# A product of the identity beside each lead step of a recurrence

## The chip, the core and the metric

The kernel runs on one core of one Trainium2 chip, in one launch, in float32. The metric is the device time of one execution in microseconds. An execution is run several times; the number quoted is the median.

## What is computed

Three layers follow one another on an input of 4 images with 128 channels and 64 x 64 pixels: a deformable neighbourhood attention (kernel lines up to about 600), a recurrence and eight state-space layers that are the subject here, and a layer of routed experts. Cut to what matters, the middle reads:

```
...
# recurrence over 4096 positions, 4 images side by side, 128 channels
z = -1
for t in range(4096):
    z = tanh(0.5 * (norm(W x1)[t] + (V/2)^T z + shift))
    x2[t] = x1[t] + 0.5 * z + 0.5
# eight layers on x2, each with 256 inner channels and 16 states
dA, dBx = exp(dt * A), dt * xc * B
h[t] = dA[t] * h[t-1] + dBx[t]
y[t] = sum over states of h[t] * C[t]
...
```

The recurrence is written here as the kernel computes it; in the reference it is a sigmoid of the same sum.

## The kernel before

The five engines each run their own queue of instructions, in the order in which the program text issues them: the kernel's order is written out by hand (`tc.manual_schedule()`), and semaphores make an instruction wait for what it reads. TensorE does the products (a weight load and a matmul pass are separate instructions, shown as PEld and PE; a float32 product comes as two of each), VectorE (DVE) the scans, ScalarE (ACT) exponentials, tanh and copies, GpSimd (POOL) elementwise products, and SyncE (SP) issues the transfers.

**The recurrence.** The class `Recurrence` holds it. `step(t)` (line 656) does one position for all four images. With every 64th position (RT = 64) it takes up the next group: a product of the identity with 256 columns of wx (line 664) puts the group's input into the PSUM tile `p`. Then, at every position, a product of `vt` (128 x 128) with the four columns of the last `z` is added into four columns of `p` (line 669), and ScalarE takes the tanh of these into the next four columns of `z` (line 672). The next step's product needs that `z`, so the steps can't overlap. In the middle of a group `load` fetches the next group's inputs; after the last position of a group POOL adds `z` to `x1` (lines 678 and 679), and SP stores it as `x2`.

**The state-space layers.** `mamba` (line 727) works on pieces ("bodies") of 512 positions, one image and one layer each, in the order piece, layer, image. A body has 16 slots; in each, two scans of 512 positions run on VectorE (line 1031), with the exponentials (line 976) on ScalarE, the inputs `dBx` from TensorE into PSUM (line 998), the products with C on POOL (line 1047) and their sum by TensorE (line 1051). The PSUM tiles of `dBx` come from the pool `psx`, which has two buffers (line 754).

**The lead.** The layers need whole pieces of 512 positions of x2. So before the loop over bodies, the function runs `PRE` = 512 + 64 = 576 steps of the recurrence by themselves. Only then come the norms of the first bodies (lines 810 to 822, 1108, 1112), and the loop, in which the other 3520 steps are spread over the slots (`STEPS`).

Of the kernel before, what the change touches and what calls it, by code (L numbers as in the profile page):

```python
# [8 lines left out]
F32 = mybir.dt.float32  # L9
# [10 lines left out]
P = 128  # L20
# [25 lines left out]
TL = 512  # L46
# [680 lines left out]
def mamba(tc, ops, I, rec, x2_d, x3_d):  # L727
# [8 lines left out]
    nc = tc.nc  # L736
# [5 lines left out]
    with ExitStack() as ctx:  # L742
# [11 lines left out]
        psx = ctx.enter_context(tc.tile_pool(name="mpx", bufs=2, space=PSUM))  # L754
# [43 lines left out]
        def load(l):  # L798
            given = wp.tile([P, W_GIVEN], F32, tag="given", name="given")
            nc.sync.dma_start(out=given, in_=I["m_given"][l])  # L800
            weights[l] = given
# [354 lines left out]
                    pieces[what](who[k])  # L1156

        load(0)
        for t in range(PRE):
            rec.step(t)  # L1160
        for s in bodies[0:3]:
            for what in ("fetch", "mean", "var", "lnv", "rstd", "u"):
                pieces[what](s)
# [363 lines left out]
@with_exitstack  # L1527
def tile_kernel(ctx: ExitStack, tc: tile.TileContext, I, out):
    nc = tc.nc
    const = ctx.enter_context(tc.tile_pool(name="const", bufs=1))  # L1530
    dram = ctx.enter_context(tc.tile_pool(name="scratch", bufs=1, space=DRAM))
    nc.scalar.preload_act_table_set(EXP_LN)
    ops = Ops(nc, const)
    stats = const.tile([P, B * NBLK, 6], F32, name="stats")
    gating_w = gating_weights(tc, const, ops, I)
    x1_d = dram.tile([P, B, L], F32, name="x1_d")
    x2_d = dram.tile([P, B, L], F32, name="x2_d")
    x3_d = dram.tile([P, B, L], F32, name="x3_d")
    wx_d = dram.tile([P, B, L], F32, name="wx_d")

    with tc.manual_schedule():
        with ExitStack() as c:
            conv_layer(tc, ops, I, x1_d, wx_d, stats)
            rec = Recurrence(c, tc, ops, I, stats, wx_d, x1_d, x2_d)
            mamba(tc, ops, I, rec, x2_d, x3_d)
        experts(tc, ops, I, gating_w, x3_d, out)
# [89 lines left out]
```

## Time and profile before

| | |
|---|---|
| median of three runs | 15757.4 us (15743.53 to 15757.71) |
| the profiled execution | 15756.73 us, of which the span from first to last instruction is 15754.2 us |
| mean clock granted to TensorE | 0.966 of full speed |
| busy share of the span | PE 91%, DVE 87%, POOL 84%, ACT 76% |

A profile line of the page's list of groups is read so: line of the kernel, engine, operation, output tile <- input tiles, output shape <- input shape, number of instructions | busy time in us, mean of one in ns | idle time of that engine before them, and what ended it. For a weight load and a matmul, "128\*128" gives the rows and columns of the array in use. A line of the timeline gives the start, the time from the first start to the last end of a run of equal instructions, engine, line, and in brackets the idle time before them. A matmul's end is modelled, and counts the time in which its results are still in the pipeline. A line of the windows view gives a stretch of the span, then for each engine its busy time and its number of instructions, then the granted TensorE clock as a share of full speed, and the transfers.

The stages, by windows of the span:

| stretch, us | PE busy | DVE busy | ACT busy | POOL busy | clock |
|---|---|---|---|---|---|
| 1400 to 1600 (attention) | 182.19 | 147.62 | 150.52 | 94.29 | 0.94 |
| 1800 to 2000 (lead steps) | 139.26 | 0.00 | 41.82 | 5.04 | 0.50 |
| 2400 to 2600 (state-space layers) | 189.97 | 186.34 | 160.52 | 186.62 | 1.00 |

### The profile page before, as it was taken

Reading aid. Unit: us, or ns where it says so; the run is one execution under the profiler, and the core shown is the slowest. Engines: PE = TensorE matmul, PEld = TensorE weight load, DVE = VectorE, ACT = ScalarE, POOL = GpSimd, SP = SyncE. Lnnn points to the kernel's source line nnn. Section 1 sums busy time; section 2 is a strip of 40 time slices with the busy share of each in tenths; the row PEclk is TensorE's granted clock in tenths of the full one; section 3 lists DMA queues with packets and bytes.
Section 4 is the critical chain, followed back from the end, with each engine's and each line's share of the span. In section 5 each row is a group of like instructions: output and inputs, shape, how many; then the busy total and the mean of one; then the engine's idle time right before and its main releaser. Section 6 shows DMA issues by size and latency. Waiting matters only on the chain. (4 is left out here: it accounts for less than half of the span.)

```text
span 15754.2 us, 303022 instructions
## 1 busy us (share of the span) xinstructions
PE 14399.4 (91%) x120596; PEld 10805.1 (69%) x120596; DVE 13692.4 (87%) x14937; ACT 12014.9 (76%) x23591; POOL 13181.8 (84%) x9086
## 2 busy tenths in 40 slices
PE   6888779999999999999999999999999999989996
PEld 3444557777777777777777777777777777766664
DVE  8998039998999899998999899989998999999994
ACT  6888247887888878877788787878887888777773
POOL 4555039999999999999999999999999999999993
PEclk8999569999999999999999999999999999999998
DMA  0000012222222222222222222222222222222224
GB/s 22 22 22 22 15 50 99 104 98 105 97 97 104 101 102 101 99 103 97 103 104 96 104 98 100 104 100 104 98 97 101 101 104 101 98 103 95 98 101 168
DMA packets 423478, 1431.58 MB, mean 91 GB/s; under 512 B 204081, under 2 KB 204465, under 8 KB 290865
## 3 DMA queue, kind: packets, MB, share of 16 engines
q1 hardware_dynamic: 422064, 1412.21, 24.1%
q8 instruction: 952, 15.60, 0.4%
q14 instruction: 462, 3.78, 0.1%
HBM read 1353.33 MB, written 58.72 MB: 90 GB/s over the span
## 5 line engine op out<-in xcount | busy, mean ns | idle before, releaser
L1031 DVE TENSOR_TENSOR_SCAN hs<-dA,state,dBx 128x512 f32<-128x512 f32 x7168 | 8716.1, 1263 | 987.2 <-PE dBx L998 865.5
L1047 POOL TENSOR_TENSOR hs<-hs,Cb 128x2048 f32<-128x2048 f32 x2048 | 9296.0, 4539 | 166.2 <-POOL state L1044 1.3
L976 ACT ACTIVATE dA<-dt,A 128x512 f32<-128x512 f32 x7168 | 4728.8, 721 | 8.2 <-DVE hs L1031 2.0
L1051 PE MATMUL yT<-ident,hs 128*128 128x128 f32 x32768 | 4328.6, 276 | 8.5 <-POOL hs L1047 8.5
L1051 PEld LDWEIGHTS yT<-ident,hs 128*128 128x128 f32 x32768 | 3779.6, 144 | 773.3 <-issue 651.1
L998 PE MATMUL dBx<-diag,dtxT 64*128 64x128 f32 x57344 | 4187.2, 285 | 72.7 <-DVE hs L1031 46.9
L998 PEld LDWEIGHTS dBx<-diag,dtxT 64*128 64x128 f32 x57344 | 3511.2, 188 | 1027.3 <-issue 697.6
L672 ACT ACTIVATE z<-p 128x4 f32<-128x4 f32 x4096 | 711.4, 174 | 1573.2 <-PE p L669 1567.3
L669 PE MATMUL p<-z,vt 128*128 128x4 f32 x8192 | 1579.5, 263 | 239.5 <-ACT z L672 233.9
L669 PEld LDWEIGHTS p<-z,vt 128*128 128x128 f32 x8192 | 1350.5, 207 | 635.6 <-ACT z L672 378.4
L1019 POOL TENSOR_TENSOR hs<-Bb,dtx 128x512 f32<-128x512 f32 x1024 | 1276.0, 1281 | 5.6 <-PE yT L1051 4.8
L1031 DVE TENSOR_TENSOR_SCAN hs<-dAp,state,hs 128x512 f32<-128x512 f32 x1024 | 1228.6, 1262 | 0.0
L863 DVE SCALAR_TENSOR_TENSOR xc<-f,taps,xc 128x509 f32<-128x509 f32 (+2 forms) x1536 | 1130.5, 736 | 42.3 <-ACT tail L858 15.1
L964 DVE TENSOR_TENSOR diag<-f,i 128x512 f32<-128x512 f32 x1792 | 1157.2, 670 | 7.8 <-PE f L952 7.8
L1044 POOL COPY state<-hs 128x4 f32<-128x4 f32 x2048 | 389.6, 190 | 773.0 <-DVE hs L1031 617.3
L1129 ACT ACT_TABLE_LOAD x771 | 989.2, 1283 | 10.5
L278 DVE SCALAR_TENSOR_TENSOR acc<-qp,dww,acc 128x512 f32<-128x512 f32 x1184 | 887.0, 749 | 12.2
L976 ACT ACTIVATE dAp<-dt,A 128x512 f32<-128x512 f32 x1024 | 709.0, 692 | 209.9 <-DVE hs L1031 178.9
L878 PE MATMUL f<-u,given 128*128 128x512 f32 x1024 | 509.9, 620 | 333.5 <-ACT pos L1097 322.8
L854 ACT ACTIVATE xc<-f,edge,taps 128x1 f32<-128x1 f32 x1536 | 426.6, 350 | 450.2 <-POOL edge L839 449.9
L937 POOL TENSOR_TENSOR dtx<-dt,xc 128x512 f32<-128x512 f32 x512 | 651.8, 1273 | 11.9 <-ACT dt L931 11.9
L947 ACT COPY dtxT<-f 128x512 f32<-128x512 f32 x512 | 298.1, 582 | 384.1 <-PE f L944 384.1
(233 smaller groups left out, 16082.2 us busy)
## 6 DMA issues: line engine op xcount, KB each, us to landing
Cb<-c_d SPq DMA_DIRECT2D x1024, 1024.0 KB, 4.6
Bb<-c_d SPq DMA_DIRECT2D x256, 512.0 KB, 5.4
given<-in_m_given_dram SPq DMA_DIRECT2D x64, 640.0 KB, 5.9
slab<-in_w_dram SPq DMA_DIRECT2D x64, 512.0 KB, 9.9
x<-x_d SPq DMA_DIRECT2D x96, 256.0 KB, 4.2
x_d<-x SPq DMA_DIRECT2D x64, 256.0 KB, 2.2
c_d<-dbl SPq DMA_DIRECT2D x512, 32.0 KB, 1.6
xb<-in_x_dram SPq DMA_DIRECT2D x32, 256.0 KB, 3.0
```

The source lines that it names most:

```text
L278: nc.vector.scalar_tensor_tensor(rows(to), x, dww[:, t : t + 1], rows(o.acc), ALU.mult, ALU.add)
L669: nc.tensor.matmul(self.p[:, k, :], self.vt, self.before, start=False, stop=True, skip_group_check=True)
L672: nc.scalar.activation(self.z[:, k, :], self.p[:, k, :], AF.Tanh, scale=0.5)
L863: nc.vector.scalar_tensor_tensor(x, o.v[h][:, : TL - k], taps[:, o.l, h, DC - 1 - k : DC - k], x, ALU.mult, ALU.add)
L964: nc.vector.tensor_tensor(o.diag[:, sp], bt.unsqueeze(2).to_broadcast([P, NB, 64, 2]), i64.unsqueeze(1).unsqueeze(3).to_broadcast([P, NB, ...
L976: nc.scalar.activation(o.dA[j][:, k, :], o.dt[h], AF.Exp, scale=A[:, o.l, h, n : n + 1])
L998: nc.tensor.matmul(o.dBx[j][:, at : at + 64, :], o.dtxT[h][row, n, :], o.diag[row, sp, n], start=True, stop=True,)
L1019: nc.gpsimd.tensor_tensor(hs[:, k, :].rearrange("p (q n t) -> p q n t", n=NB, q=2), o.Bb[:, k, :].rearrange("p (q n t) -> p q n t", n=NB, ...
L1031: nc.vector.tensor_tensor_scan(hs[:, k, :], o.dA[j][:, k, :], hs[:, k, :] if sp == SP_B else o.dBx[j][:, :, k], state[:, o.l, o.b, h, s : ...
L1047: nc.gpsimd.tensor_tensor(hs, hs, o.Cb[f], ALU.mult)
L1051: nc.tensor.matmul(o.yT[:, n, :], x[:, n * P : (n + 1) * P], ops.ident, start=start and n == 0, stop=True, is_transpose=True, skip_group_c ...
L1129: return lambda o: nc.scalar.preload_act_table_set(name)
```

## The change

After each of the 576 lead steps, TensorE is given one more product: 32 columns of the identity as the weights, and the whole identity, 128 columns, as the data that moves through. The result goes to a corner of a tile `idle` in one of the two `dBx` buffers in PSUM. The tile is allocated once, ahead of the lead steps, and nothing reads it. The steps inside the loop over bodies are as before.

```diff
@@ -1156,8 +1156,13 @@
         load(0)
+
+        idle = psx.tile([P, 2, TL], F32, tag="dBx", name="idle")
         for t in range(PRE):
             rec.step(t)
+            nc.tensor.matmul(
+                idle[0:32, 0, 0:P], ops.ident[:, 0:32], ops.ident, start=True, stop=True
+            )
         for s in bodies[0:3]:
```

## The prediction

> **What bounds the kernel now.** I read the page first, for the stretch that the change touches.
>
> ```profile
> span 15754.2 us, 303022 instructions
> ...
> POOL 4555039999999999999999999999999999999993
> PEclk8999569999999999999999999999999999999998
> ...
> L672 ACT ACTIVATE z<-p 128x4 f32<-128x4 f32 x4096 | 711.4, 174 | 1573.2 <-PE p L669 1567.3
> L669 PE MATMUL p<-z,vt 128*128 128x4 f32 x8192 | 1579.5, 263 | 239.5 <-ACT z L672 233.9
> ```
>
> Each digit is a slice of 394 us. In the slices where POOL drops to 0 the clock of TensorE (PEclk) is at 5 to 6 tenths: these are the lead steps of the recurrence, which run alone. The windows view gives the clock and the load in the middle of them:
>
> ```profile
> 1800.00:2000.00 200.00, 139.26 (x469) 118.18 (x469) 0.00 (x0) 41.82 (x234) 5.04 (x8) 0.50 0.04 8
> ```
>
> The columns are length, busy time of PE, weight loads, DVE, ACT and POOL, then the clock: 0.50, with DVE idle. The timeline shows one step, then a step that opens a new group of 64 and has the product of the identity with wx (L664) ahead of its own:
>
> ```profile
> 1700.71 0.17 ACT L672 ACTIVATE z<-p 128x4 f32<-128x4 f32 x1 [0.68 <-PE p L669]
> 1700.93 0.50 PEld L669 LDWEIGHTS p<-z,vt 128*128 128x128 f32 x2 [0.35 <-ACT z L672]
> 1700.93 0.59 PE L669 MATMUL p<-z,vt 128*128 128x4 f32 x2 [0.26 <-ACT z L672]
> 1701.56 0.17 ACT L672 ACTIVATE z<-p 128x4 f32<-128x4 f32 x1 [0.68 <-PE p L669]
> ```
>
> ```profile
> 1715.21 0.17 ACT L672 ACTIVATE z<-p 128x4 f32<-128x4 f32 x1 [0.68 <-PE p L669]
> 1715.44 0.50 PEld L664 LDWEIGHTS p<-wx,ident 128*128 128x128 f32 x2 [0.35 <-ACT z L672]
> 1715.44 1.23 PE L664 MATMUL p<-wx,ident 128*128 128x256 f32 x2 [0.26 <-ACT z L672]
> ...
> 1716.05 0.75 PEld L669 LDWEIGHTS p<-z,vt 128*128 128x128 f32 x2
> 1716.49 0.40 PE L669 MATMUL p<-z,vt 128*128 128x4 f32 x2
> ...
> 1716.93 0.17 ACT L672 ACTIVATE z<-p 128x4 f32<-128x4 f32 x1 [1.54 <-PE p L669]
> ```
>
> So a lead step is a strict ring: two loads and two passes of the product (0.59 us), 0.04 us to ScalarE, tanh 0.17, 0.05 back. The tanh starts 0.85 us apart (1700.71, 1701.56). 567 such steps and nine with L664 (1716.93 - 1715.21 = 1.72 us) make 567 x 0.853 + 9 x 1.72 = 499 us, and the first product of a step starts at 1660.6, the result of the last group is taken up by POOL at 2159.7. All of that lies on the path: nothing else runs, and the scans wait for the first 512 positions.
>
> **What a faster clock would be worth.** Among the scans, at clock 1.00, the same pair reads
>
> ```profile
> 4003.28 0.39 PE L669 MATMUL p<-z,vt 128*128 128x4 f32 x2
> ```
>
> against 0.59: 0.20 us a step, and tanh takes 0.17 at either clock (mean 174 ns on the page). A step would be 0.65 us, and 576 x 0.20 = 115 us would be gained. The change decides on this through one question: do its products bring the clock up?
>
> **What the change adds.** Each lead step gets one more product behind its own: two weight loads of 32 columns and two passes of 128 columns (all f32 products in the trace come as two). It removes nothing, adds no DMA, no wait, and nothing for ACT, DVE, POOL or SP; the tile it writes is never read. 576 x 2 = 1152 loads and as many passes on TensorE.
>
> Cost of a pass: four passes of 512 columns at half clock take 3.78 us (L306 below); the last one's end is counted about 0.36 us late (a 4-column pass, which streams next to nothing, has a mean of 364 ns in this stretch), so (3.78 - 0.37) / 4 = 0.853 us for 512 columns and 0.213 for 128. The two passes occupy the array for 0.43 us, at full clock for half that. The nearest row for the load is L1482, which has just this shape (128 rows, 32 columns, 128 moved): loads of 106 to 178 ns.
>
> Where it goes: the step's second pass has left the array at 0.59 - 0.35 = 0.24 us after the step's start, and the next step's first load waits for tanh until 0.853, its first pass some 0.15 later still. In between 0.178 + 0.43 = 0.61 us of new work ends at 0.85. The nearest row says that a load runs beside a product in flight: L669's loads start at 1716.05, while L664 lasts to 1716.67, and that group step is longer by 1.72 - 0.85 = 0.87 us, which is its two passes of 256 columns (0.853) and almost nothing for loads. So I take **0** for the delay. The cover is tanh with its two hand-overs; were it gone, the bounds are: below, 0, since the chain of the step itself loses nothing by a product behind it; above, a next load that must wait until the new product is out of the pipeline: 0.24 + 0.18 + 0.43 + 0.35 (the late end) = 1.20, or 0.35 us a step and 200 us in all. A gain can come by the clock only.
>
> **Whether the clock rises.** Windows cut where the clock changes, 3.41 us each, from the stage before (same columns), and TensorE's timeline there:
>
> ```profile
> 681.28:684.69 3.41, 2.77 (x4) 1.17 (x4) 3.38 (x7) 3.38 (x4) 0.00 (x0) 0.50 0.00 0
> 684.69:688.10 3.41, 3.41 (x31) 2.03 (x30) 1.74 (x3) 2.71 (x4) 2.25 (x3) 0.50 0.00 0
> 688.10:691.51 3.41, 3.41 (x16) 1.68 (x15) 1.70 (x6) 2.66 (x9) 3.31 (x3) 1.00 0.02 5
> ```
>
> ```profile
> 681.92 3.78 PE L306 MATMUL po<-on,offw 128*128 128x512 f32 x4 [2.46 <-ACT on L295]
> ```
>
> In the first window 512-column passes stream from about 682.08 (0.16 for the first load) to its end: 2.61 of 3.41 us, 76%. The window after it is still at 0.50. That one is busy throughout, and the third is at 1.00. In the trace I find windows at half clock that raised the next one from 79% streaming on (2186.55 to 2189.96, where L818 and L849 stream some 2.7 us), and practically none below 75%; weight loads do not seem to count, since the lead steps are 59% loads (118.18 of 200) and stay at 0.50. A changed lead step streams 0.43 of 0.853 us: **50%**, 52% with its own passes. A window with an L664 in it comes to about (0.853 + 0.43 + 2 x 0.43) / 3.41 = 63%. Both are short of 76%. That it loads 32 columns only is taken as no difference; I see no reason why it should count for more than a full one. So the clock stays at 0.50, and the sum is 0: span 15754.2, time 15756.7 as in the profiled run, which had 2.5 us around its span; the median of the three runs is 15757.4.
>
> The Trainium skill, page "TensorE: Matmul & The Clock Gate", section "HAM oscillation — how this bites in real kernels", holds against this that the clock falls only over gaps in TensorE's work longer than about 3.4 us; by that the changed steps, with gaps of a few tenths, run at full clock, and the sum is 15757 - 115 = 15642. The lead steps of this trace already have gaps of 0.26 us only and sit at 0.50 for 500 us, so I go by how much is streamed, not by the gaps.
>
> **Rivals.**
> - *The clock rises.* For it: 52% is far above the 2% streamed now, the 0.36 us that a pass is in flight beyond its streaming is counted as nothing here, and with the new product TensorE has something in flight nearly all the time. Against it: the 76% window above, which is 81% busy. It is 15642; if the clock can't hold, since at full clock the streaming is 0.22 of 0.65 us (34%), and it goes up and down in turn, half of it, 15700.
> - *The product stands in the way.* One mechanism: the next step's first load, in TensorE's queue behind the new second pass, has to wait for it. The place is the ring PE, ACT, PE; behind that load stand the step's passes, and tanh waits for these. It decides once the new product holds the array beyond 0.853 us after the step's start; to be seen at all (31.5 us) it needs 0.055 us a step. In the middle of its bounds it costs 0.17 x 576 = 100 us: 15857; at the upper one 15957. For it: my 0.85 fits with nothing to spare if loads do not overlap. Against it: the row at 1716.05.
> - *The change does nothing that lasts beyond the lead*: it moves the two-buffer tile dBx on by one, which is the other buffer for each product and no wait. This is part of my forecast.
>
> **How the numbers follow.** A change under 0.2% (31.5 us) can't be told from none here; the three runs alone differ by 14 us. My forecast of no rise and no delay has 0.66, the risen clock 0.20 (0.12 held, 0.08 in turns), the blocked load 0.14. The time is that of the first, 15757 us, its own range 15740 to 15786 (the lowest run, and 0.05 us a step of delay). To leave no more than 2 in 10 out the range takes in the risen clock, 15642, with some us for a gain at the seams: 15635 to 15790; the blocked load stays outside. Faster 0.20, same 0.66, slower 0.14.
>
> **What would show it.** Right: the windows between 1660 and 2160 still read 0.50, the step is still 0.85 us from tanh to tanh, L669's pair still takes 0.59, and the new line appears with some 0.43 us more of PE busy time in each step. Wrong by the clock: windows of 1.00 in the lead and pairs of 0.39. Wrong by the queue: clock 0.50, steps above 0.90, and L669's loads waiting for PE instead of for ACT z.

## The result

The changed kernel takes 15893.5 us (median of 4 runs, 15889.21 to 15897.62) against 15756.98 before: a ratio of 1.0087, 95% interval 1.0075 to 1.0099, or 136 us more. The forecast was no change, and the range ended at 15790.

The page after, its lines that answer to those shown of before:

```profile
PEclk8999559999999999999999999999999999999998
...
L672 ACT ACTIVATE z<-p 128x4 f32<-128x4 f32 x4096 | 710.7, 174 | 1704.8 <-PE p L669 1698.7
```

The clock did not rise: two slices are now at 5 tenths. ScalarE's wait for the recurrence's product grew from 1567.3 to 1698.7 us, by 131 us. The windows view of the lead (length, busy time of PE, weight loads, DVE, ACT, POOL, then the clock):

```profile
1800.00:2000.00 200.00, 200.00 (x734) 126.36 (x734) 0.00 (x0) 32.97 (x185) 3.77 (x6) 0.50 0.03 6
```

In 200 us there are 185 instructions of ScalarE where there were 234, and TensorE counts as busy all the time. The timeline of one step, with the added product in L1163:

```profile
1801.11 0.17 ACT L672 ACTIVATE z<-p 128x4 f32<-128x4 f32 x1 [0.91 <-PE p L669]
1801.57 0.50 PEld L669 LDWEIGHTS p<-z,vt 128*128 128x128 f32 x2 [0.38 <-ACT z L672]
1801.57 0.59 PE L669 MATMUL p<-z,vt 128*128 128x4 f32 x2
1802.09 0.18 PEld L1163 LDWEIGHTS idle<-ident 128*32 128x32 f32 x2
1802.09 0.64 PE L1163 MATMUL idle<-ident 128*32 128x128 f32 x2
1802.19 0.17 ACT L672 ACTIVATE z<-p 128x4 f32<-128x4 f32 x1 [0.91 <-PE p L669]
1802.65 0.50 PEld L669 LDWEIGHTS p<-z,vt 128*128 128x128 f32 x2 [0.38 <-ACT z L672]
```

A step takes 1.08 us (1801.11 to 1802.19) instead of 0.85. The tanh ends at 1802.36, and the next load used to follow 0.05 us later; now it comes at 1802.65. The wait is still written down as one for ScalarE (the last semaphore that the load waits for), but ScalarE had been done for 0.29 us: it is the added product that the load waits for. Two more times are worth noting. The added product's own load starts at 1802.09, 0.07 us before the counted end of the step's product (1801.57 + 0.59 = 2.16); the step's next load starts at 1802.65, 0.08 before the counted end of the added one (1802.09 + 0.64 = 2.73). Each load sits at the end of the product ahead of it. Over five steps (1800.02 to 1805.45) the step is 1.086 us, 0.233 more than before, and 576 x 0.233 = 134 us is the whole of the loss.

### The profile page after: what moved, and what is told of

Same layout as the page of the kernel before. It is cut to its first block, busy times and chain, and to the rows that moved or that the text cites. A ratio compares the mean times of both kernels' runs of the same rounds, so it can differ in the third digit from the quotient of the medians.

```text
span 15894.1 us, 305326 instructions
## 1 busy us (share of the span) xinstructions
PE 14694.6 (92%) x121748; PEld 10921.4 (69%) x121748; DVE 13691.2 (86%) x14937; ACT 12008.9 (76%) x23591; POOL 13173.2 (83%) x9086
## 5 line engine op out<-in xcount | busy, mean ns | idle before, releaser
L672 ACT ACTIVATE z<-p 128x4 f32<-128x4 f32 x4096 | 710.7, 174 | 1704.8 <-PE p L669 1698.7
L669 PEld LDWEIGHTS p<-z,vt 128*128 128x128 f32 x8192 | 1350.5, 207 | 650.6 <-ACT z L672 393.8
L669 PE MATMUL p<-z,vt 128*128 128x4 f32 x8192 | 1580.4, 263 | 87.1 <-ACT z L672 79.1
```

Source lines behind the costliest of these rows:

```text
L669: nc.tensor.matmul(self.p[:, k, :], self.vt, self.before, start=False, stop=True, skip_group_check=True)
L672: nc.scalar.activation(self.z[:, k, :], self.p[:, k, :], AF.Tanh, scale=0.5)
```

## The experiments

The theory T formed on this: a load waits when the product ahead of it used another width of the array (32 columns of weights after 128, or 128 after 32); between equal widths it runs beside that product. The rivals: any product in that place blocks the next load (S); an added product costs a fixed time (Q). For the clock: the streaming count of the prediction (the share of a window of 3.41 us in which columns move through the array), made into one number, 77% of a window at half clock or 38% at full, against the rule that only long gaps in TensorE's work matter (G). In the kernels below only the added product differs from the changed kernel.

**The full width of weights**

```diff
-                idle[0:32, 0, 0:P], ops.ident[:, 0:32], ops.ident, start=True, stop=True
+                idle[:, 0, 0:P], ops.ident, ops.ident, start=True, stop=True
```

> The added product takes all 128 columns of the identity as weights instead of 32; 128 columns still move. Theory T (tiling: a load for another width of the array, 32 columns after 128 or 128 after 32, waits until the product before it has left the array; between equal widths it runs beside that product): no width changes in a step any more, the step is back at 0.85 us, clock 0.50, time 15757 +- 20. Rival S (any product behind the step's own stands in the way of the next load, whatever its width): step 1.09 us, 15894.

15757.49 us (10 runs), ratio to before 1.0001, interval 0.9991 to 1.0010. The timeline and the windows view:

```profile
1800.33 0.17 ACT L672 ACTIVATE z<-p 128x4 f32<-128x4 f32 x1 [0.68 <-PE p L669]
...
1801.01 0.77 PE L1163 MATMUL idle<-ident 128*128 128x128 f32 x2
1801.18 0.17 ACT L672 ACTIVATE z<-p 128x4 f32<-128x4 f32 x1 [0.68 <-PE p L669]
1801.41 0.50 PEld L669 LDWEIGHTS p<-z,vt 128*128 128x128 f32 x2
1801.57 0.43 PE L669 MATMUL p<-z,vt 128*128 128x4 f32 x2
```

```profile
1800.00:2000.00 200.00, 200.00 (x933) 199.29 (x932) 0.00 (x0) 41.93 (x235) 3.76 (x6) 0.50 0.03 7
```

A product with four times the weights costs nothing. The next load starts at 1801.41, 0.37 us before the counted end of the added product (1801.01 + 0.77) and 0.06 after tanh; the step is 0.85 us again. S is out. The second view also speaks against G: TensorE counts as busy for 200.00 of 200 us, without a gap that the profile shows, and the clock is at 0.50.

**The narrow weights, with 4 columns moved**

```diff
-                idle[0:32, 0, 0:P], ops.ident[:, 0:32], ops.ident, start=True, stop=True
+                idle[0:32, 0, 0:4], ops.ident[:, 0:32], ops.ident[:, 0:4], start=True, stop=True
```

> The weights keep their 32 columns, but only 4 columns move instead of 128. Theory T: both changes of width remain, the load of the added product still comes 0.28 us after the step's second pass, but its own passes take 0.01 instead of 0.43 us, so it is out of the array before tanh is done: step 0.85 to 0.88 us, 15757 to 15775. Rival Q (an added product costs a fixed time in TensorE's queue, whatever its size): step 1.09 us, 15894.

One run, 15765.36 us, against runs of before on the same chip up to 15760.25. In the timeline:

```profile
1800.74 0.18 PEld L1163 LDWEIGHTS idle<-ident 128*32 128x32 f32 x2
1800.74 0.27 PE L1163 MATMUL idle<-ident 128*32 128x4 f32 x2
...
1801.08 0.50 PEld L669 LDWEIGHTS p<-z,vt 128*128 128x128 f32 x2
```

The added load still comes late, 0.52 us after the step's first load (1800.22), but the product ends at 1801.01, ahead of the 1801.08 at which the step could go on anyway. The step is 0.85 us: the first wait is there, and tanh hides it. Of the second nothing can be seen, since by the same 0.07 us it would be over at 1800.94, before tanh is done. Q is out.

**64 columns of weights**

```diff
-                idle[0:32, 0, 0:P], ops.ident[:, 0:32], ops.ident, start=True, stop=True
+                idle[0:64, 0, 0:P], ops.ident[:, 0:64], ops.ident, start=True, stop=True
```

> 64 columns of the identity as weights, 128 moved. Theory T: 128, 64, 128 is a change of width just as 128, 32, 128 is; both loads wait; step 1.07 to 1.10 us, 15880 to 15900. Rival W (the wait grows with how narrow the product is): step 0.95 to 1.0, 15815 to 15845.

One run, 15922.27 us: 29 us above the changed kernel, so the loss does not shrink towards the full width; W is out, and T's own numbers were 0.04 us a step too low.

```profile
1801.01 0.59 PE L669 MATMUL p<-z,vt 128*128 128x4 f32 x2
1801.53 0.29 PEld L1163 LDWEIGHTS idle<-ident 128*64 128x64 f32 x2
1801.53 0.69 PE L1163 MATMUL idle<-ident 128*64 128x128 f32 x2
...
1802.15 0.50 PEld L669 LDWEIGHTS p<-z,vt 128*128 128x128 f32 x2 [0.33 <-ACT z L672]
```

Again both loads start 0.07 us before the counted end of the product ahead (1801.60 and 2.22). What I had left out is that a wider pair of loads, 0.29 instead of 0.18 us, makes the product longer (0.69 instead of 0.64).

One more rival, that a narrow product holds up any load behind it, whatever its width, is ruled out by the changed kernel itself. The added product is two loads and two passes of 32 columns; its loads take 0.18 us together (the line of 1802.09) and one of its passes 0.42 us, and in the trace the second load starts 0.40 us ahead of the first pass's counted end. The trace of the kernel before says the same throughout, for rows as for columns. Of some 8000 loads whose size (rows and columns of the array, rounded up to 32, 64 or 128) differs from that of the pass ahead, none starts more than 0.073 us ahead of that pass's counted end; of some 112 000 of equal size 98% do, half of them by 0.27 us or more.

**256 and 160 columns moved, full width of weights**

```diff
-                idle[0:32, 0, 0:P], ops.ident[:, 0:32], ops.ident, start=True, stop=True
+                idle[:, 0, 0 : 2 * n].rearrange("p (a b) -> p a b", a=2), ops.ident,
+                ops.ident[:, 0:n].unsqueeze(1).to_broadcast([P, 2, n]), start=True, stop=True
```

with n = 128 in the first and n = 80 in the second (n stands here for the number in the kernels).

> 128 columns of weights, 256 columns moved. Streaming theory (the clock is at full in the next window when a window of 3.41 us streams some 77% at half clock, or 38% at full clock, which is the same work): at half clock the product streams 0.85 us in a step of about 0.9 to 1.1, over 77%, so the clock rises in the first windows; at full clock it streams 0.43 of 0.65 us and holds. Step 0.65 us, 15640 +- 15. Rival (such a product doesn't move the clock): clock 0.50, steps of 0.9 us or more, 15785 or more.

> 128 columns of weights, 160 columns moved. Streaming theory: 0.55 of 0.85 us, 64%, is short of 77%; clock 0.50, step 0.85 us, 15757 +- 20. Rival G (the clock rises when TensorE has no long gaps): clock 1.00 as with 256 columns, step 0.65, 15640.

256 columns: 15679.37 us (4 runs), ratio 0.9952, interval 0.9937 to 0.9967; faster, but 40 us short of what was expected. 160 columns: one run, 15819.87 us, clock 0.50 throughout, which is against G, but 60 us slower than expected. Both misses have one cause. With 128 columns the step's own product already follows the added one with no room between them: at full width it starts at 1801.57, 0.21 us before the added one's counted end (1801.78), and 0.21 us is what a pass of 128 columns lasts beyond its streaming (0.422 in the changed kernel, less 0.213). So each column more adds its streaming to the step: at 0.853 us for 512 columns, 1.67 ns each, 2 x 32 x 1.67 ns = 0.107 us gives 0.96 us with 160 columns, 2 x 128 x 1.67 = 0.43 gives 1.28 with 256, and these are the steps measured (tanh at 1800.93 and 1801.89 with 160 columns, at 1740.92 and 1742.20 with 256). The windows view with 160 columns:

```profile
1800.00:2000.00 200.00, 200.00 (x830) 199.31 (x830) 0.00 (x0) 37.20 (x209) 3.78 (x6) 0.50 0.03 6
```

So the product of 256 columns streams 0.85 + 0.01 of 1.28 us, 68% and not the 77% that I had counted on, and the clock stays down at first. The windows view of that kernel where it comes up, and a later stretch:

```profile
1743.51:1746.92 3.41, 3.41 (x11) 2.81 (x12) 0.00 (x0) 0.34 (x3) 1.26 (x2) 0.50 0.15 32
1746.92:1750.34 3.42, 3.42 (x21) 2.86 (x22) 0.00 (x0) 0.92 (x6) 0.00 (x0) 1.00 0.37 83
1800.00:2000.00 200.00, 200.00 (x1209) 159.94 (x1208) 0.00 (x0) 54.44 (x305) 5.04 (x8) 1.00 0.04 9
```

The windows before it, at 65 to 70%, had left the clock at 0.50. The window from 1743.51 holds the first L664 since the lead's first step, with 0.85 us of streaming in place of a wait, and comes to 76% by the same count; the next one is at full clock, and so is the rest of the lead, since 0.43 of 0.655 us is 66%, far over 38%. The lead had run for some 85 us at half clock and 1.28 us a step by then, and 64 steps at 1.28 instead of 0.655 us are the 40 us that the gain lacks.

**A wide start, then 160, 128 or 256 columns**

```diff
+            a, n = (4, 128) if t < 10 else (2, 80)
-                idle[0:32, 0, 0:P], ops.ident[:, 0:32], ops.ident, start=True, stop=True
+                idle[:, 0, 0 : a * n].rearrange("p (a b) -> p a b", a=a), ops.ident,
+                ops.ident[:, 0:n].unsqueeze(1).to_broadcast([P, a, n]), start=True, stop=True
```

with (2, 64) in the second and (2, 128) in the third.

> 128 columns of weights throughout; 512 columns moved in the first 10 lead steps, 160 in the others. Streaming theory: the wide products stream about 80% of the time at half clock, the clock rises within some 15 us; after that 0.27 of 0.65 us, 42%, is streamed at full clock, over the 38% that hold it there. Steps 0.65 us to the end of the lead, 15645 +- 15. Rival (the 77% that raise the clock are needed to hold it too): it falls back at once to 0.50 with steps of 0.96, 15820 as with 160 columns alone.

> As the one before, but 128 columns after the first 10 lead steps: 0.22 of 0.65 us, 35%, is under the 38%. Streaming theory: the clock rises with the wide products and falls back soon after them, steps 0.85 us for most of the lead, 15755 +- 20. Rival (once risen, the clock stays up as long as TensorE has no long gap): 15645.

> 512 columns moved in the first 10 lead steps, 256 in the others, weights of 128 columns. With 256 alone the clock stayed at 0.50 for 92 us, until a window with the product of wx in it. Streaming theory: with the wide products it rises within some 15 us; then as before 0.655 us a step. 15645 +- 15, some 30 us under 256 columns alone, and about 110 under the kernel before.

| after 10 steps of 512 columns | median, us | ratio to before | 95% interval |
|---|---|---|---|
| 160 columns (5 runs) | 15651.09 | 0.9932 | 0.9919 to 0.9944 |
| 128 columns (10 runs) | 15760.23 | 1.0004 | 0.9994 to 1.0013 |
| 256 columns (5 runs) | 15649.71 | 0.9931 | 0.9919 to 0.9944 |

All three fall where the streaming count put them. The windows of the first, from the start of the lead:

```profile
1657.97:1661.38 3.41, 3.41 (x9) 2.15 (x8) 1.66 (x4) 0.51 (x3) 0.00 (x0) 0.50 0.89 266
1661.38:1664.79 3.41, 3.41 (x13) 1.81 (x12) 0.00 (x0) 0.53 (x3) 0.00 (x0) 1.00 0.00 1
...
1800.00:2000.00 200.00, 200.00 (x1220) 159.29 (x1220) 0.00 (x0) 55.26 (x307) 5.05 (x8) 1.00 0.04 9
```

One window with the product of wx and the first wide ones raises the clock (the next one is at 1.00), and 160 columns, which alone never raise it, hold it to the end of the lead. With 128 columns after the same start:

```profile
1676.84:1680.25 3.41, 3.41 (x22) 2.73 (x22) 0.00 (x0) 1.01 (x6) 0.00 (x0) 1.00 0.00 0
1680.25:1683.66 3.41, 3.41 (x17) 3.31 (x16) 0.00 (x0) 0.70 (x5) 0.00 (x0) 0.50 0.00 0
1800.00:2000.00 200.00, 200.00 (x931) 199.06 (x929) 0.00 (x0) 42.23 (x234) 5.04 (x8) 0.50 0.03 7
```

The first window that holds nothing but 128-column steps at full clock (1676.84, 35%) is the last one at full clock. PE reads 3.41 of 3.41 us in all these windows, so its busy time tells nothing here. The best two kernels are 101 to 102 us under the one before and some 243 under the changed one; between them there is no difference.

## Why the prediction was wrong

- **What bounds the lead** was right: the ring of product, hand-over, tanh, hand-over is the path, and a change of 0.233 us in it came out whole at the end, 134 of 136 us.
- **Whether the clock rises** was right, and the reason given, too little streaming, held in the lead of every kernel here. The changed kernel stays at 0.50 with some 40% (0.43 of its longer step of 1.086 us; the 50% were reckoned on a step of 0.853), as do the kernels with 52% (128 columns, full width) and some 57% streaming (160 columns); 68% is not enough. The windows that raised the clock with 256 columns (from 1743.51) and after the wide start (from 1657.97) come to about 76%, and so does the one of the prediction that did not (681.28, before), so the bound is known to a few per cent only.
- **The delay of the next load** is the step that failed. "The nearest row says that a load runs beside a product in flight: L669's loads start at 1716.05, while L664 lasts to 1716.67 ... So I take 0 for the delay." That row has L669 behind L664, both with 128 columns of weights. The added product has 32, and I took its width for a matter of load time only. The row that was nearest in what counts stands in the timeline of before, in the attention, where a product of 32 columns is followed by one of 128:

```profile
1633.10 0.38 PE L432 MATMUL pa<-at,vk 110*32 110x128 f32 x2
1633.41 0.14 PEld L440 LDWEIGHTS pa<-ident,rx 128*128 128x128 f32 x1 [0.20 <-issue]
1633.42 0.33 PE L440 MATMUL pa<-ident,rx 128*128 128x128 f32 x1
1633.42 0.36 PEld L463 LDWEIGHTS po<-qp,rwo 128*128 128x128 f32 x2
```

  L440's load starts 0.07 us before the counted end of L432 (1633.48) after 0.20 us in which nothing that the profile knows is waited for; the next load, L463's, of the same width, starts together with L440's product. With it the step follows: the added load at 0.59 - 0.07 = 0.52, the product 0.64 long as measured, the next load at 0.52 + 0.64 - 0.07 = 1.09 us.
- **The bounds** were right and not used: the upper one was 0.35 us a step, and the measured 0.233 lies inside. Its terms were not those of the wait: the added load starts at 0.52 and not at 0.24, and a pass of 128 columns lasts 0.21 us beyond its streaming and not 0.35 (that figure was read off a pass of 4 columns, whose 364 ns seem to hold a wait for its weights; the narrow passes of 4 columns take 0.27 us for two). The rival "the product stands in the way" had the place and the sign, at 100 us in the middle and 0.14 of the chance, but the range went to the other side and stopped at 15790.
- **The worth of a faster clock**, 0.20 us a step and 115 us, was nearly right: with the clock at full the steps are 0.65 us, and after the wide start the lead with 160 columns takes 386 us from its first tanh to its last, where it took 498. That is 112 us less, of which the medians show 101.
- **The 0.85 us** at which the new work was said to end, "with nothing to spare", came out for the full width by luck. There the added columns are through 1.01 us after the step's first load (1800.56 to 1801.57), not 0.85; but the next step's own columns, too, start only at 1.01, since its load comes at 0.85, runs beside the added product and takes 0.16 more. So 128 columns cost nothing, and 160 cost 0.107 us a step.

## What to carry to other kernels

Before putting filler work behind a product on a serial path, look in the trace for a pair of neighbours that change the width of the array as the filler does; a row with the same shapes is not enough if the neighbour differs. Work out what share of a 3.41 us window the passes stream, not how busy TensorE looks: here the border at half clock was about 76% (68% did not raise the clock), and at full clock 42% held it and 35% did not. Where the sustained work is enough to hold but not to raise, a short wide start does the raising.

## What the runs showed of the hardware

- A weight load of another width than the product ahead started 0.07 us before that product's counted end in the changed kernel, with 64 columns, and in the kernel before; of the same width it started 0.37 us before it in the kernel with 128 columns at full width.
- The clock has two stable readings for one and the same work: the product of 160 columns ran at 0.50 through the whole lead by itself, and at 1.00 after ten wide steps.
- The Trainium skill, page "TensorE: Matmul & The Clock Gate", section "HAM oscillation — how this bites in real kernels", ties the fall of the clock to gaps in TensorE's work above some 3.4 us. The trace disagrees: with 128 columns at full width TensorE showed no gap in 200 us and stayed at 0.50, and after the wide start it fell from 1.00 to 0.50 with no gap that the profile shows (1676.84 to 1683.66).
- How the count treats a product on part of the array was not tried, since in the changed kernel either reading stays under the limit. The kernel before has windows that speak against counting it in full. This one, in the attention, streams some 53% by the count (L243, L410 and L379, 1.82 of 3.41 us), and yet the next one is at half clock:

```profile
664.21:667.62 3.41, 2.42 (x12) 1.18 (x10) 3.41 (x9) 3.40 (x8) 2.46 (x2) 1.00 0.71 226
667.62:671.03 3.41, 3.41 (x5) 1.16 (x4) 3.41 (x8) 1.01 (x3) 0.70 (x3) 0.50 0.00 0
```

  More than half of this streaming is L379, which uses 32 of the 128 rows. Were its passes to count by a quarter, the window would come to some 31%, which is an estimate that no run here tests.
